# Zero products under the first loads, halved first loads, moments by piece, and a shorter inverse square root

## The chip, the cores and the metric

The kernel runs on one core of one Trainium2 chip. The metric is the device time of one execution in microseconds. The kernel before was timed three times: 1588.16, 1591.35 and 1591.58 us, a median of 1591.35 us. One more execution was recorded by the profiler; all profile lines in this document that are said to be of before come from that one.

The core has five engines with an instruction stream each: TensorE (PE in the profile; its weight loads are PEld), VectorE (DVE), ScalarE (ACT), GpSimd (POOL) and SyncE (SP), which here issues most of the transfers. An engine executes its own stream in order and waits for others by semaphores.

## The reference

The input is x of shape (4, 1024, 256) in float32, 4096 tokens of 256 values. Two layers follow, each of a mixing part and a feed-forward part, and each part is wrapped in a residual sum and a layer norm without scale and shift:

```
x = layernorm(x + L0_attn(x))   # state-space mixing, 2 heads of 128, state 64
x = layernorm(x + L0_ffn(x))    # 256 -> 1024, exact GELU, -> 256
x = layernorm(x + L1_attn(x))   # 16 heads of 16, 64 positive features, causal linear attention
x = layernorm(x + L1_ffn(x))    # 2 shared experts, and 2 of 8 routed experts per token, SiLU-gated, hidden 512
layernorm(x) = (x - mean) / sqrt(var + 1e-5)      over the 256 values of a token
L1_attn:  q, k are divided by max(norm, 1e-12) per head before the features
```

Four layer norms and the norms of q and k each need an inverse square root; these are what the changed function `rsqrt` computes. The first mixing part starts with `dtBC = x @ W_xproj.T`, the first matrix product of the program.

## The kernel before, in words

**Tiling.** Tokens are cut into NBLK = 8 blocks of TB = 512, a block into NT = 4 tiles of P = 128 tokens. `xs[i]` holds block i with tokens on the partitions (128 x 4 x 256) and is updated in place through all parts; `xts[i]` holds its transpose from the host (128 x 2 x 512), of which only the first products make use. Everything is float32. PE executes such a product of 512 columns as two instructions, and the profile counts both.

**Order of the work.** PE's instructions stand in an order that the program writes out: each piece of work is a `Task` with an assumed cost, a rank and waiting times behind others, and `trace_tasks` (line 243) picks the next one by these. The streams of the other engines in that stage are put in order by the compiler's scheduler, from its own estimate of each instruction's time. So DVE, ACT and POOL streams can change in places that a diff does not touch, while PE's does not. In the last stage (from line 1239) PE, DVE and ACT all keep the written order.

**Opening (lines 119 to 175).** SP issues, in order: the weights `wx_sb` (128 x 2 x 2 x 128: chunk of the 256 input values, product number, column), `xts[0]`, the small vector `vec0` copied to all partitions, `xts[2]`, `xts[4]`, `xts[6]`, the even `xs`, and the rest. ACT loads a function table and computes `neg_a` (line 172), which needs `vec0`. `ssd_block` (line 269) then begins with `project(0)` and `project(1)` (line 283), two products each that add up over the two chunks k; ACT copies each result out of PSUM (line 285), and `steps` (line 287) turns the first with four transposes into `ps_dtb` (line 291). DVE works out the step sizes from it (lines 299 to 312).

**Inverse square roots.** `rsqrt(v, shape, tag)` (line 178) takes a first estimate from the bits of v (a shift, line 182, and a subtraction from a constant, line 183) and improves it with three Newton steps of three DVE instructions each (lines 185 to 187). It is called 49 times: by `layernorm` (line 206) 24 times on 128 x 4 values, after the first mixing, the first feed-forward part and the attention, once for each block; by `attn_front` (line 508) 16 times on 128 x 64 values; and by `last_norm` (line 1064) 9 times on 128 x 4, 128 x 3 or 128 x 1 values. Each instruction needs the one before.

**After the first layer.** Attention (`attn_front`, `attn_back`, `attn_tail`) runs interleaved with the first feed-forward part of other blocks and with the shared experts (`shared_jobs`, line 920). Then tokens are sorted by expert, and the routed part (`slot_tiles`, line 998) runs 71 tiles of 128 tokens, whose results are added into `acc` in memory.

**Last stage (lines 1239 to 1268).** `combine` (line 1058) loads each block's part of `acc` back and POOL adds it to `xs[i]` (line 1062), eight times. Meanwhile PE runs the shared experts for the blocks 6 and 7: for each block eight `hidden` pieces (ps_g, line 938; SiLU on ACT, line 946; product on DVE, line 947) and four `output` pieces (ps_e, line 956; added to x on DVE, line 965). The counter n numbers these pieces, 0 to 23; the pieces 20 to 23 are the outputs of block 7's four tiles. The last norms are spread between the pieces: `last_norm(i, tiles)` gives three functions, `sums` (two DVE instructions for each tile: moments, lines 1075 and 1076), `scales` (lines 1080 to 1082, with `rsqrt`) and `finish` (ACT, line 1086, and the store, line 1090). Blocks 0 to 6 take one function after each of three pieces. For block 7 the first three tiles' `sums` and `scales` come after piece 22, `finish` after piece 23, and then the fourth tile is done by itself.

The functions that the change touches, and what calls them:

## Time and profile before

| what | value |
|---|---|
| median of three runs | 1591.35 us (1588.16 to 1591.58) |
| the profiled execution | 1590.25 us |
| its span, first to last instruction | 1588.5 us |
| mean granted PE clock | 0.988 of full |
| PE, DVE, ACT, POOL busy, share of the span | 95%, 48%, 38%, 35% |
| instructions of DVE | 2383 |
| PE's first product | at 5.06 us |

The profile's page gives the busy time of each engine, the span in forty slices, the chain of work that ended last (followed back from the last instruction, at each step to what released it) and the costliest groups of instructions. A timeline gives start and duration of each instruction and, in brackets, how long its engine was idle before it and what ended the wait. The granted clock is what the throttle let PE have, in parts of full speed. DVE instructions overlap their neighbours a little, so what counts for a chain of dependent ones is the time from start to start.

### The profile page before, as it was taken

The numbers are of one execution on the slowest core, as the hardware profiler recorded it, in microseconds if no ns is written. First come the engines' busy times: TensorE is split into PE (matmuls) and PEld (weight loads), VectorE is DVE, ScalarE is ACT, GpSimd is POOL, SyncE is SP. The second block draws the span as 40 slices with busy tenths as digits, with TensorE's granted clock in tenths as the row PEclk, the third lists the DMA queues.
The fourth block names the chain that finished last, engine by engine and source line by source line (L and its number), as shares of the span: only waits on it lengthen the run. The fifth ranks groups of instructions, "written<-read, shape, count | busy, mean of one in ns | idle before, by whom it ended". The sixth has DMA issues, their size and how long they took to land.

```text
span 1588.5 us, 25546 instructions
## 1 busy us (share of the span) xinstructions
PE 1505.6 (95%) x9744; PEld 973.1 (61%) x9744; DVE 768.2 (48%) x2383; ACT 600.9 (38%) x1061; POOL 557.8 (35%) x531
## 2 busy tenths in 40 slices
PE   8999989999998999899999999999999999999987
PEld 5575655656675767565667565565666666666544
DVE  6977824763656556655544437122222222222374
ACT  2555374354556363554545621102222222222132
POOL 5623323343433162614332204013444444443410
PEclk9999999999999999999999999999999999999999
DMA  9200000000000000200001034042322322322421
GB/s 345 85 1 1 1 1 1 14 15 1 27 2 14 15 1 28 94 28 15 28 2 41 2 105 160 14 143 38 47 46 45 47 46 45 47 45 33 123 73 47
DMA packets 48023, 74.08 MB, mean 47 GB/s; under 512 B 8512, under 2 KB 38464, under 8 KB 46368
## 3 DMA queue, kind: packets, MB, share of 16 engines
q1 hardware_dynamic: 33840, 52.19, 9.3%
q0 software_dynamic: 13632, 18.69, 7.6%
q8 instruction: 80, 1.31, 0.4%
q10 hardware_dynamic: 432, 1.57, 0.3%
q14 instruction: 39, 0.32, 0.1%
HBM read 46.19 MB, written 26.25 MB: 46 GB/s over the span
## 4 chain that ended last, share of the span: by engine, by line
PE 73%; DVE 13%; ACT 8%; POOL 3%; issue 2%; DMA 1%; SPq 0%; DVEq 0%; ACTq 0%; POOLq 0%
PE ps_ge L1008 15%; PE ps_g L938 9%; PE ps_ye L1030 8%; PE ps_e L956 6%; PE ps_h L436 5%; PE ps_f L448 5%; PE ps_sc L611 3%; PE ps_o L650 3%; PE ps_qk L497 2%; PE ps_gT L1023 2%; PE ps_bc L283 2%; PE ps_v L522 1%; PE ps_k L633 1%; PE ps_p L559 1%; PE ps_w L715 1%
## 5 line engine op out<-in xcount | busy, mean ns | idle before, releaser
L1008 PE MATMUL ps_ge<-w,xeT 128*128 x568 | 255.7, 593 | 1.0 <-issue 1.0
L938 PE MATMUL ps_g<-xTs,w 128*128 128x512 f32 x512 | 230.8, 603 | 12.6 <-ACT sl L946 6.7
L938 PEld LDWEIGHTS ps_g<-xTs,w 128*128 128x128 f32 x512 | 95.9, 192 | 126.1 <-issue 105.5
L1008 PEld LDWEIGHTS ps_ge<-w,xeT 128*128 128x128 f32 x568 | 102.4, 190 | 103.5 <-issue 103.5
L1039 POOL DMA_INDIRECT acc<-ye,back x71 | 112.5, 1584 | 112.2 <-DVE xew L995 77.0
L436 PE MATMUL ps_h<-xT,w_sb 128*128 128x512 f32 x256 | 125.3, 632 | 22.6 <-ACT hT L439 12.0
L983 POOL DMA_INDIRECT xe<-xt,sent x71 | 70.0, 986 | 216.6 <-PE ps_xe L991 154.1
L1018 DVE TENSOR_TENSOR ge<-se,ps_ge 128x512 f32<-128x512 f32 x71 | 48.8, 688 | 183.9 <-PE ps_ge L1008 181.0
L1030 PE MATMUL ps_ye<-w2e,geT 128*128 x568 | 134.4, 380 | 0.0
L956 PE MATMUL ps_e<-w,gT 128*128 128x256 f32 x512 | 116.7, 385 | 5.8 <-DVE x L965 3.0
L448 PE MATMUL ps_f<-w_sb,hT 128*128 128x256 f32 x512 | 118.1, 385 | 1.6 <-ACT hT L439 1.6
L956 PEld LDWEIGHTS ps_e<-w,gT 128*128 128x128 f32 x512 | 97.4, 193 | 24.3 <-DVE x L965 4.6
L1030 PEld LDWEIGHTS ps_ye<-w2e,geT 128*128 128x128 f32 x568 | 102.5, 190 | 12.2 <-ACT ye L1038 0.8
L448 PEld LDWEIGHTS ps_f<-w_sb,hT 128*128 128x128 f32 x512 | 96.6, 192 | 17.1 <-issue 2.8
L947 DVE TENSOR_TENSOR gT<-sl,ps_g 128x512 f32<-128x512 f32 x64 | 43.7, 686 | 118.3 <-PE ps_g L938 86.6
L436 PEld LDWEIGHTS ps_h<-xT,w_sb 128*128 128x128 f32 x256 | 49.1, 201 | 79.6 <-issue 49.9
L946 ACT ACTIVATE sl<-ps_g 128x512 f32<-128x512 f32 x64 | 37.9, 595 | 147.7 <-PE ps_g L938 138.8
L623 DVE TENSOR_TENSOR sc<-ps_sc,mask_le 128x512 f32<-128x512 f32 x96 | 62.6, 685 | 60.4 <-PE ps_sc L611 51.3
L1016 ACT ACTIVATE se<-ps_ge 128x512 f32<-128x512 f32 x71 | 42.4, 597 | 125.0 <-PE ps_ge L1008 125.0
L572 POOL TENSOR_SCALAR qf<-qf,csq 128x512 f32<-128x512 f32 x32 | 50.2, 1570 | 107.6 <-ACT qf L570 106.5
L621 POOL TENSOR_TENSOR sc<-sc,mask_le 128x512 f32<-128x512 f32 x32 | 40.9, 1279 | 113.9 <-ACT sc L620 113.6
L577 POOL TENSOR_SCALAR qf<-qf,csq 128x512 f32<-128x512 f32 x32 | 65.2, 2038 | 15.9 <-ACT qf L575 13.0
(251 smaller groups left out, 2578.1 us busy)
## 6 DMA issues: line engine op xcount, KB each, us to landing
w<-in_moe SPq DMA_DIRECT2D x8, 1024.0 KB, 8.7
xt<-in_xT SPq DMA_DIRECT2D x8, 512.0 KB, 9.9
x<-in_x SPq DMA_DIRECT2D x8, 512.0 KB, 10.3
acc<-zero SPq DMA_DIRECT2D x16, 256.0 KB, 4.8
xt<-x SPq DMA_DIRECT2D x8, 512.0 KB, 3.6
td<-xTr SPq DMA_DIRECT2D x16, 256.0 KB, 2.5
w2e<-in_moe SPq DMA_DIRECT2D x8, 512.0 KB, 7.4
part<-acc SPq DMA_DIRECT2D x8, 512.0 KB, 7.2
```

The lines of the kernel that those rows point to most:

```text
L436: nc.tensor.matmul(ps, w1_sb[:, k, m * P : (m + 1) * P], v.xT[:, k, :], start=(k == 0), stop=(k == KC - 1))
L448: nc.tensor.matmul(v.ps[:, j % 2, :], v.hT[:, m, j * P : (j + 1) * P], w2_sb[:, m, :], start=(m == 0), stop=(m == HID0 // P - 1),)
L572: nc.gpsimd.tensor_scalar_mul(f, f, csq)
L577: nc.gpsimd.tensor_scalar(f, f, CLIP_LO, csq, ALU.max, ALU.mult)
L623: nc.vector.tensor_mul(t_s, ps_s, mask)
L938: nc.tensor.matmul(ps[s], w[e][:, 2 * s + k, m * P : (m + 1) * P], xT[i][:, k, :], start=(k == 0), stop=(k == KC - 1),)
L956: nc.tensor.matmul(ps, gT[i, e][:, m, j * P : (j + 1) * P], w2e[:, m, :], start=(e == 0 and m == 0), stop=(e == NSH - 1 and m == HID // P ...
L983: nc.gpsimd.indirect_dma_start(out=xe, out_offset=None, in_=xt, in_offset=bass.IndirectOffsetOnAxis(ap=sent[:, s : s + 1], axis=0),)
L1008: nc.tensor.matmul(pg[a], xeT[s][:, k, :], w13[:, bass.ds(e * (4 * HID) + (2 * a + k) * HID, HID)], start=(k == 0), stop=(k == KC - 1),)
L1018: nc.vector.tensor_mul(ge[s], se, pg[1])
L1030: nc.tensor.matmul(ps[:, :D], geT[s][:, m, :], w2[:, bass.ds(of[s] * (2 * HID) + m * D, D)], start=(m == 0), stop=(m == HID // P - 1),)
L1039: nc.gpsimd.indirect_dma_start(out=acc, out_offset=bass.IndirectOffsetOnAxis(ap=back[:, s : s + 1], axis=0), in_=ye, in_offset=None, compu ...
```

## The change

There are four parts.

1. PE's stream gets two products of a tile of zeros (128 x 512, set by DVE) with itself, ahead of the first `ssd_block`; their result is never read.
2. The loads of `wx_sb` and `xts[0]` are halved. `wx_sb` is halved by product number, and the first half is issued on ACT; `xts[0]` is halved by chunk. In the built program ACT issues its half before the table load, and SP issues `xts[0]` chunk 0, `wx_sb` second half, `xts[0]` chunk 1, then `vec0` and the rest as before.
3. `rsqrt` takes after the same first estimate one step of third order and one Newton step, in nine DVE instructions altogether instead of eleven. A scale factor of 0.375 that the first step leaves out is put into the second step's constants.
4. The moments of the last block's first three tiles are taken one by one after the pieces 20, 21 and 22, instead of all three after 22. For that `last_norm` gets a flag `split`.

```diff
-    nc.sync.dma_start(out=wx_sb, in_=wx)
-    nc.sync.dma_start(out=xts[0], in_=xT[0])
+    for n in range(2):
+        (nc.scalar, nc.sync)[n].dma_start(out=wx_sb[:, :, n, :], in_=wx[:, :, n, :])
+        nc.sync.dma_start(out=xts[0][:, n, :], in_=xT[0][:, n, :])
     nc.sync.dma_start(out=vec0, in_=vecs[:NVEC0].partition_broadcast(P))
...
         nc.vector.tensor_scalar(r.bitcast(I32), s.bitcast(I32), -1.0, float(0x5F3759DF), ALU.mult, ALU.add)
-        for _ in range(3):
-            nc.vector.scalar_tensor_tensor(s, r, -0.5, r, ALU.mult, ALU.mult)
-            nc.vector.tensor_mul(s, s, v)
-            nc.vector.scalar_tensor_tensor(r, s, 1.5, r, ALU.add, ALU.mult)
+        nc.vector.tensor_mul(s, r, r)
+        nc.vector.tensor_mul(s, s, v)
+        nc.vector.scalar_tensor_tensor(s, s, -10.0 / 3.0, s, ALU.add, ALU.mult)
+        nc.vector.scalar_tensor_tensor(r, s, 5.0, r, ALU.add, ALU.mult)
+        nc.vector.scalar_tensor_tensor(s, r, -0.5 * 0.375**3, r, ALU.mult, ALU.mult)
+        nc.vector.tensor_mul(s, s, v)
+        nc.vector.scalar_tensor_tensor(r, s, 1.5 * 0.375, r, ALU.add, ALU.mult)
         return r
...
-    def last_norm(i, tiles):
+    def last_norm(i, tiles, split=False):
...
+        st = sm.tile([P, NT, 6], F32, tag="ln_st", name=f"ln_st{i}_{tiles[0]}")
+
         def sums():
-            st = sm.tile([P, NT, 6], F32, tag="ln_st", name=f"ln_st{i}_{tiles[0]}")
             for k, j in enumerate(tiles):
-                nc.vector.bn_stats(st[:, k, :], xs[i][:, j, :])
-                nc.vector.bn_aggr(mv[:, k, :], st[:, k, :])
+                moments(k, j)
+
+        def moments(k, j):
+            nc.vector.bn_stats(st[:, k, :], xs[i][:, j, :])
+            nc.vector.bn_aggr(mv[:, k, :], st[:, k, :])
...
+        if split:
+            return moments, scales, finish
         return sums, scales, finish
...
     with tc.manual_schedule(engines={mybir.EngineType.PE}):
+
+        idle = wkf.tile([P, TB], F32, name="idle")
+        nc.vector.memset(idle, 0.0)
+        ps = bank("ps_idle", 0)
+        for _ in range(2):
+            nc.tensor.matmul(ps, idle[:, :P], idle, start=True, stop=True)
         for i in range(NBLK):
             ssd_block(i, wk0)
...
+            if n == 20:
+                ends = last_norm(NBLK - 1, whole[:-1], True)
+            if 20 <= n < 23:
+                ends[0](n - 20, n - 20)
             if n == 22:
-                ends = last_norm(NBLK - 1, whole[:-1])
-                ends[0]()
                 ends[1]()
```

## The prediction

> **What bounds the kernel now.** I read the page first: busy time, then the chain that ended last. TensorE (PE) is busy for 95% of the span, and most of the chain is its work; the other engines come in only where PE waits.

> ```profile
> PE 1505.6 (95%) x9744; PEld 973.1 (61%) x9744; DVE 768.2 (48%) x2383; ACT 600.9 (38%) x1061; POOL 557.8 (35%) x531
> PE 73%; DVE 13%; ACT 8%; POOL 3%; issue 2%; DMA 1%; SPq 0%; DVEq 0%; ACTq 0%; POOLq 0%
> ```

> So the change can win only some 80 us of PE waits, or slow-clock PE time. It touches four stretches. First the timeline of the opening (start, duration, engine, line):

> ```profile
> 1.25 0.42 SPq L120 DMA_DIRECT2D xt<-in_xT  x1
> 5.06 5.83 PE L283 MATMUL ps_bc<-xt,wx_sb 128*128 128x512 f32 x8 [5.06 <-DMA xt<-in_xT]
> 7.75 0.33 PEld L283 LDWEIGHTS ps_bc<-xt,wx_sb 128*128 128x128 f32 x1 [0.52 <-issue]
> 7.99 0.20 ACT L172 ACTIVATE neg_a<-vec 128x2 f32<-128x2 f32 x1 [5.92 <-DMA vec<-in_vecs]
> 8.61 0.33 PEld L283 LDWEIGHTS ps_bc<-xt,wx_sb 128*128 128x128 f32 x1 [0.52 <-issue]
> 8.85 0.58 ACT L285 COPY bc<-ps_bc 128x512 f32<-128x512 f32 x1 [0.65 <-PE ps_bc L283]
> 9.44 0.19 PEld L283 LDWEIGHTS ps_bc<-xt,wx_sb 128*128 128x128 f32 x1 [0.50 <-issue]
> 9.87 0.19 PEld L283 LDWEIGHTS ps_bc<-xt,wx_sb 128*128 128x128 f32 x1 [0.24 <-issue]
> ```

> To see: PE waits 5.06 us for the load; its instructions then come 0.86 us apart (7.75 to 8.61) and only from 9.44 on 0.43 apart. A weight load takes 0.33 us before, 0.19 after. That is half clock, although the page's clock row says 9 there. ACT's first copy stands behind `neg_a`, which waits for the small vector load until 7.99.

> Then the stretch after the routed part, where POOL adds eight times (2.34 us each, 1497.81 to 1516.28):

> ```profile
> 1511.74 2.26 DVE L185 SCALAR_TENSOR_TENSOR ln_s<-ln_r 128x4 f32<-128x4 f32 x1
> 1514.04 2.26 DVE L186 TENSOR_TENSOR ln_s<-ln_s,ln_v 128x4 f32<-128x4 f32 x1
> 1516.33 0.16 DVE L187 SCALAR_TENSOR_TENSOR ln_r<-ln_s,ln_r 128x4 f32<-128x4 f32 x1
> 1517.79 0.69 DVE L947 TENSOR_TENSOR gT<-sl,ps_g 128x512 f32<-128x512 f32 x1
> 1518.53 3.45 PE L938 MATMUL ps_g<-xTs,w 128*128 128x512 f32 x4 [5.21 <-DVE gT L947]
> ```

> A 0.16 us step of the inverse square root lasts 2.26 us while POOL adds; PE waits 5.21 us for the product queued behind, then runs 4 instructions at half clock (granted clock 0.52 from 1518 to 1520).

> Last the chain at the end (start, length):

> ```profile
> 1577.36 0.34 DVE ln_st L1075
> 1579.00 0.18 DVE ln_v L1080
> 1581.54 0.34 DVE x L965
> 1585.10 0.60 ACT x L1086
> ```

> From 1577.36 the end hangs on DVE alone: three pairs of moments, a root, the last add, one more pair, one more root.

> **The change, part by part.** The sum is made against the profiled execution: 1590.25 us (span 1588.5), 1.1 below the median 1591.35 of runs from 1588.16 to 1591.58.

> *Start.* Removed: half clock. Added: a DVE memset of 128x512 ahead of two small ones that nobody needs before 930 us. Nearest rows: POOL's memset of that size 0.51 us, DVE's two of 128x16 0.11; taking 0.5, it ends at 0.86+0.5 = 1.4. PE's two zero products are four instructions of 0.86: 1.5 to 4.9. The loads: wx landed at 3.6, xt at 4.92; the halves bring the same bytes, but the last is issued a slot later (1.72 for 1.25), so it lands at 5.4 at worst. If the clock is up by then, the eight real instructions need 8x0.43 = 3.4 us and end near 8.4, not 10.89. When is it up? After the two slow starts shown, 3.1 us (1518.5 to 1521.6) to 4.4 us (5.06 to 9.44) after the first instruction: 4.6 to 5.9. But the vector load is now SP's fourth issue, 2.18 for 1.72, so `neg_a` runs at 8.45 at worst, ACT's copy at 8.7 to 9.3, and PE's `ps_dtb` transposes start at 9.3 instead of 10.89: -1.5. Ends: -2.1 (five slow instructions x 0.43, all kept), +0.5 (one issue slot late, nothing won). Next late is xt2, landing at 9.3 and now perhaps 9.8, when PE wants it at 9.75: no further gain, no loss. The load issued on ACT (0.4 us by SP's row) pushes its 1.28 us table load to 2.5; ACT waits until 8 anyway. Later loads go out 0.46 later; PE's only wait for a load in the whole trace is the first, so 0. Each load's issue waits for the one eight earlier; for the first x load that is now the first load, landed long before it is due.

> [...]

> *Roots.* 49 calls (24 norms of two layers, 16 of q and k, 9 last) have 9 DVE instructions for 11. A dependent step costs 0.20 us from start to start at 128x4, 0.26 at 128x64, so 0.4 to 0.5 a call. Over all 49 that is some 20 us of DVE, of which only what lies on the path counts. Adding up the chain's pieces on lines 182 to 187 before 900 us: 169 pieces, 37.4 us, of which 11 long ones held by POOL take 11.6, the other 158 take 25.8. POOL's holds do not shrink. 2/11 of 25.8 is 4.7 us if all of it reached PE. Half is my value, -2.4: there PE waits 22 us on DVE in some eighteen gaps (3.67 at 255, 1.96 at 491), but several end on ACT right behind, and interleaved steps cost only 0.07 of chain each. Against it stands the scheduler's new order on ACT, by the built program: near 63, 128 and 149 us a norm's four ACT instructions (2.07) go ahead of a decay, a copy and a Gelu. At 149 the Gelu `hT` ends at 151.7 for 149.1, just when PE wants its bank (151.8); the next decay slips by 0.3. At 128 the step chain behind the copy starts 0.6 later. At 63 the decay's consumer waits until 67.15 anyway. POOL swaps `qk` scaling ahead of one `qf` scaling at 717 and 808; `qkn_r` is ready there (715.2, 805.3): 0. Ends for this part: -5.5 (all 4.7 and some 0.8 by order) and +2.1 (no gain, one norm in front of PE).

> *After the routed part.* During POOL's adds the same five steps are held; multiplies are held as line 186 shows. After 1516.3 six remain instead of eight: -0.39 for `gT` and PE's wait. The next root (1521.4 to 1523.5) is also before what PE waits for at 1526.81 (1.38 us): again -0.39. Together -0.8; ends -0.4 and -2.3 (if the shorter wait also spares the half-clock stretch, 3.1x0.48 = 1.5).

> *End.* Two pairs of moments (0.53 each) move to where DVE idles 3.8 and 3.0 us; were that cover gone, each add would slip 0.6. The three tiles' scales are then done at 1580.1 for 1581.5, before PE's last product (1577.42+3.72 = 1581.14): the last add starts at 1581.2 for 1581.46, -0.3; the last root -0.4. Together -0.7 (ends -0.4, -1.1). The 3.4 us from 1585.10 to the end stay.

> Sum: -1.5 -2.4 -0.8 -0.7 = -5.4: 1590.25-5.4 = **1584.9 us**.

> **Rivals.**
> 1. The middle gives nothing: 1587.3, with the norm ahead of the Gelu up to 1589.4. For it: DVE is in order, the 11 holds remain, ACT ends 12.0 us of PE's waits on `hT`. Against: 255, where only norm steps and two clamps stand before `xT`.
> 2. Zero products do not raise the clock, or too late: start 0 instead of -1.5, 1586.4. For: no row shows PE on zeros. Against: the clock rose within 4.4 us of work both times.
> 3. Half-clock stretches go as well. The granted clock falls in 11 stretches, 19.1 us lost by the 3 us windows after the start, 1.7 each. Two or three shorter waits sparing it: 1580.5.
> 4. Slower: the clock falls at more places. It fell after waits of 0.43 and 0.39 us (764, 765) and of 0.29 and 0.81 (344, 346) but not after 2.05 (369) or 1.96 (491), so which gap trips it hangs on where the gap falls, and every gap moves now. Each costs 1.7; it decides from five extra stretches (8.6 us), 1593.4 and up. For: twelve waits over 1.3 us stand where the clock held. Against: the runs before spread by 3.4 us only.

> **How the numbers follow.** My case 0.50, rival 1 0.24, rival 2 0.09, rival 3 0.10, rival 4 0.07. About 0.2%, 3.2 us, is what a measurement of this kernel tells from no change: faster means below 1588.2. My case, 2 and 3 are faster and of rival 1 its better end, 0.06; same is the rest of rival 1; slower is rival 4. The range 1580.3 to 1589.6 takes in rivals 1, 2 and 3 and leaves out rival 4 and the far ends of the sums; the start's and middle's unknowns make its width.

> **What would show it.** `ps_dtb` first at 9.3 (10.1 if the clock is late, 10.9 if zeros do nothing), instructions 0.43 apart from 6 on; PE's wait near 1518 at 4.8 for 5.2; last add directly behind PE; steps at 255 and 166 to 191 shorter, and total PE waits before 900 down by 2 to 3 us. Wrong it would be by new waits of `ps_h` for `hT` near 145, or more windows with a clock near 0.5.

## The result

The change makes the kernel a little faster. In the first comparison the median is 1583.86 us (1582.07 to 1584.61, 6 runs) against 1588.65 before (1588.16 to 1591.58, 6 runs), a ratio of 0.9963 with an interval of 0.9950 to 0.9976. Measured again, beside three of the experiments, it was 1581.90 against 1589.67: 0.9951 (0.9937 to 0.9965). The forecast was 1584.9 with a range of 1580.3 to 1589.6. The profiled execution took 1583.58 us (span 1581.9), 6.67 less than the one before.

The page of the changed kernel, its busy times and the shares of the chain that ended last:

```profile
PE 1507.4 (95%) x9748; PEld 973.6 (62%) x9748; DVE 753.6 (48%) x2286; ACT 601.8 (38%) x1061; POOL 557.9 (35%) x531
...
PE 75%; DVE 12%; ACT 8%; POOL 2%; issue 1%; DMA 0%; DVEq 0%; ACTq 0%; POOLq 0%
```

PE's time without work, span less busy time, falls from 82.9 to 74.5 us. Of these 8.4, 3.6 are the zeros, which now fill PE's first wait (1.51 to 5.08); the rest is waits that have gone. DVE has 97 instructions fewer (two a root, one memset more).

The opening (start, duration, engine, line; what the idle time before it ended on):

```profile
1.51 3.78 PE L1154 MATMUL ps_idle<-idle 128*128 128x512 f32 x4 [1.51 <-DVE run L850]
1.97 0.58 SPq L121 DMA_DIRECT2D xt<-in_xT  x1
...
4.23 0.34 PEld L288 LDWEIGHTS ps_bc<-xt,wx_sb 128*128 128x128 f32 x1 [0.52 <-DMA wx_sb<-in_wx]
...
6.42 0.71 PEld L288 LDWEIGHTS ps_bc<-xt,wx_sb 128*128 128x128 f32 x2 [1.00 <-DMA xt<-in_xT]
7.59 0.19 PEld L288 LDWEIGHTS ps_bc<-xt,wx_sb 128*128 128x128 f32 x1 [0.47 <-issue]
...
8.69 0.20 ACT L173 ACTIVATE neg_a<-vec 128x2 f32<-128x2 f32 x1 [5.93 <-DMA vec<-in_vecs]
...
9.74 0.60 PE L296 MATMUL ps_dtb<-ident,bc 128*128 128x128 f32 x4
```

PE is busy from 1.51, but waits for the second half of the x load until 6.42. Weight loads are short, that is, the clock is up, only from 7.59, and `neg_a` still waits for the vector load. `ps_dtb` starts at 9.74; before it was 10.72.

After the routed part, and at the end:

```profile
1508.96 2.27 DVE L187 TENSOR_TENSOR ln_s<-ln_s,ln_v 128x4 f32<-128x4 f32 x1
1511.26 0.16 DVE L188 SCALAR_TENSOR_TENSOR ln_s<-ln_s 128x4 f32<-128x4 f32 x1
...
1512.32 0.69 DVE L952 TENSOR_TENSOR gT<-sl,ps_g 128x512 f32<-128x512 f32 x1
...
1513.06 3.54 PE L943 MATMUL ps_g<-xTs,w 128*128 128x512 f32 x4 [4.57 <-DVE gT L952]
...
1575.33 0.42 DVE L970 TENSOR_TENSOR x<-ps_e,x 128x256 f32<-128x256 f32 x1 [0.96 <-PE ps_e L961]
...
1578.58 0.60 ACT L1095 ACTIVATE x<-x,ln_v,ln_r 128x256 f32<-128x256 f32 x1 [2.54 <-DVE ln_v L1091]
```

As many steps as before are held by POOL, but fewer remain behind, so PE waits 4.57 us for 5.21; the four products behind still run at half clock (3.54 us; granted clock 0.50 from 1513 to 1515). At the end the last add now waits for PE (0.96) and not for DVE's moments.

How far the changed kernel is ahead at the same PE instruction (its start before less its start after; the places are times of the changed kernel): 1.0 us at `ps_dtb`, 1.8 at 136, 3.25 at 188, 4.9 at 225, 6.55 at 527; then it loses 1.5 at 561 and 0.5 at 633, stays at 4.8 to 4.9 up to 1489, and gains 1.0 behind the routed part and 0.75 at the end. The 1.7 us from 188 to 225 are half clock that the profile before has there and this one has not.

### The profile page after: what moved, and what is told of

It is laid out like the page before. It is cut to its first block, busy times and chain, and to the rows that moved or that the text cites. A ratio compares the mean times of both kernels' runs of the same rounds, so it can differ in the third digit from the quotient of the medians.

```text
span 1581.9 us, 25458 instructions
## 1 busy us (share of the span) xinstructions
PE 1507.4 (95%) x9748; PEld 973.6 (62%) x9748; DVE 753.6 (48%) x2286; ACT 601.8 (38%) x1061; POOL 557.9 (35%) x531
## 4 chain that ended last, share of the span: by engine, by line
PE 75%; DVE 12%; ACT 8%; POOL 2%; issue 1%; DMA 0%; DVEq 0%; ACTq 0%; POOLq 0%
PE ps_ge L1013 15%; PE ps_g L943 10%; PE ps_ye L1035 8%; PE ps_e L961 6%; PE ps_h L441 5%; PE ps_f L453 5%; PE ps_o L655 3%; PE ps_sc L616 3%; PE ps_qk L502 2%; PE ps_gT L1028 2%; PE ps_v L527 2%; PE ps_bc L288 2%; PE ps_k L638 1%; PE ps_p L564 1%; PE ps_w L720 1%
## 5 line engine op out<-in xcount | busy, mean ns | idle before, releaser
L951 ACT ACTIVATE sl<-ps_g 128x512 f32<-128x512 f32 x64 | 38.0, 597 | 149.1 <-PE ps_g L943 140.0
## 6 DMA issues: line engine op xcount, KB each, us to landing
xt<-in_xT SPq DMA_DIRECT2D x7, 512.0 KB, 10.9
```

## The experiments

All times are medians; "before" was run beside each group and stood at 1589.65, 1589.67, 1590.02 and 1590.12 us in the four groups. Single executions of one kernel differ by several us (those of before lay between 1585.4 and 1596.1), so a profile shows where time goes, and only the medians what a kernel takes.

### One part at a time

**The start alone.** The kernel before, with the halved loads and

```diff
+        idle = wkf.tile([P, TB], F32, name="idle")
+        nc.vector.memset(idle, 0.0)
+        ps = bank("ps_idle", 0)
+        for _ in range(2):
+            nc.tensor.matmul(ps, idle[:, :P], idle, start=True, stop=True)
```

> The kernel before with the zero products and the split loads alone; roots and moments as before. Theory (the middle's gain comes from shorter roots): the first ps_dtb transposes start at 9.7 us for 10.7, and this lead of 1.0 us is carried to the end or partly lost in the first waits; time 0.5 to 1.3 us below before, waits before 900 us as before. Rival (the middle's gain is one of moved gaps, set off by the earlier start): the lead grows to 3 us or more by 320 us although the roots are old, because other waits fall and the half-clock stretch near 222 us goes; time 3 us or more below before.

Measured: 1587.63 us, ratio 0.9988 (0.9975 to 1.0001). `ps_dtb` started at 10.36, not 9.74, because the vector load landed later in this execution (`neg_a` at 9.54 for 8.69). The lead does not grow to 3 us in the middle: up to 1489 us it is 2.1 at most, and 1.7 of that are half clock that the profile before has behind 138 us and this one has not. By the medians the start is worth 2.0 us, by the interval anything from 4 us to nothing, and the lead at `ps_dtb` is 0.4 us in this profile.

**The roots alone.** The kernel before with the nine-instruction root in place of

```diff
-        for _ in range(3):
-            nc.vector.scalar_tensor_tensor(s, r, -0.5, r, ALU.mult, ALU.mult)
-            nc.vector.tensor_mul(s, s, v)
-            nc.vector.scalar_tensor_tensor(r, s, 1.5, r, ALU.add, ALU.mult)
```

> The kernel before with the new inverse square root alone; opening and moments as before. Theory: the parts add up, so this gives the middle's -3.9 us (lead of 1.5 between 166 and 191 us, and the half-clock stretch near 222 us gone), -0.9 after the routed part and -0.4 at the end, in all about -5 us, ps_dtb still at 10.7. Rival: without the earlier start the gaps fall elsewhere, the half-clock stretch near 222 stays, and the losses of 1.5 us at 561 and 0.5 us at 633 stay or grow: -1 to -3 us.

Measured: 1582.70 us, ratio 0.9956 (0.9940 to 0.9973). As far as the intervals tell, that is all of the gain; this one reaches from 4.3 to 9.5 us and takes in the theory's 5. Where the time leaves the path is the same as in the whole change: near 190, 225, 345 and 501 us (times of the kernel before), with the same losses at 566 (1.46) and 637 (0.51).

**The moments alone** (the `split` flag of `last_norm`, its callers as changed):

> The kernel before with the last tiles' moments by piece alone. Theory: the three pairs of moments leave the end's chain, but the old root is 0.4 us longer, so the last add starts directly or nearly directly behind PE: -0.2 to -0.4 us, and nothing before 1560 us is changed: PE's instructions start at the same times within 0.1 us up to there. Rival: the moments by piece each sit ahead of an add that PE or ACT waits for, and the end is later by up to 0.6 us.

Measured: 1589.98 us, ratio 0.9997 (0.9983 to 1.0011). No gain of 0.2 to 0.4 us can be seen in the median or excluded at this width. The profile's end did as foretold: the last add starts 0.42 us after the start of PE's last instruction, where it was 0.70. But with the roots alone it is 0.42 too, so that beside the shorter root the moments bring nothing that the profiles show. The expectation that nothing moves before 1560 us was wrong for one execution against another: with the same order up to there this profile is 5 us ahead at the end, since four half-clock stretches of the profile before (138, 222, 717 and 765 us) were missing in it and one more came (311).

**The change without zeros** (the tile and its memset go too)

```diff
-        for _ in range(2):
-            nc.tensor.matmul(ps, idle[:, :P], idle, start=True, stop=True)
```

> The changed kernel without the products of zeros and their memset; split loads, roots and moments as changed. Theory: the zeros raise the clock, so without them the first eight real instructions all or nearly all run 0.86 us apart, full clock from about 9 us on, ps_dtb at 10.5 to 11 us for 9.74, and the time is 0.8 to 1.2 us above the changed kernel. Rival (the second half of the x load and neg_a set the start, the zeros add little): ps_dtb at 9.7 to 10.0 all the same, and the same time within 0.3 us.

Measured: 1581.32 us, ratio 0.9947 (0.9926 to 0.9968). The clock and `ps_dtb` were later than the theory said, and yet the time is not higher. The opening without zeros:

```profile
4.09 2.08 PE L288 MATMUL ps_bc<-xt,wx_sb 128*128 128x512 f32 x2 [4.09 <-DMA wx_sb<-in_wx]
...
6.79 5.49 PE L288 MATMUL ps_bc<-xt,wx_sb 128*128 128x512 f32 x6 [0.62 <-DMA xt<-in_xT]
...
12.07 0.92 PE L296 MATMUL ps_dtb<-ident,bc 128*128 128x128 f32 x4
```

`ps_dtb` is at 12.07, 1.35 later than before the change: the halved loads bring PE's first work forward to 4.09, but the last half lands at 6.8, where the whole load had landed by 5.06, and the products behind it still start slow (0.86 us apart up to 12.07).

### Which half of the opening, and how much a step is worth

Four kernels on one chip: the changed one, the one with the opening as before, the one with whole loads and zeros, and the one with a still shorter root.

```diff
 f2_opening:  - zeros; - halves;  + nc.sync.dma_start(out=wx_sb, in_=wx) and (out=xts[0], in_=xT[0])
 f3_whole:    - halves;           + nc.sync.dma_start(out=wx_sb, in_=wx) and (out=xts[0], in_=xT[0])
 f4_two_newton, in rsqrt:
-        (the seven lines of the two new steps)
+        for _ in range(2):
+            nc.vector.scalar_tensor_tensor(s, r, -0.5, r, ALU.mult, ALU.mult)
+            nc.vector.tensor_mul(s, s, v)
+            nc.vector.scalar_tensor_tensor(r, s, 1.5, r, ALU.add, ALU.mult)
```

> The changed kernel itself, to stand beside the three others on one chip. Both theories: about 0.35 to 0.45% below before, 1582.5 to 1584.5 us; the start's transposes ps_dtb between 9.7 and 10.4 us, by when the vector load and the second half of the x load land.

> The changed kernel with the opening as before: no zero products, whole loads; new roots and moments by piece. Theory (the roots are nearly all of it, and the opening is worth what ps_dtb shows, 0.4 to 1.4 us): ps_dtb at 10.7 to 11.5 us, and the time 0.4 to 1.4 us above the changed kernel. Rival (the opening's shift is absorbed by the first waits between 50 and 200 us): the same time as the changed kernel within 0.4 us.

> The changed kernel with the first two loads whole again, zero products kept. Theory (the split delays the last piece, 6.4 to 6.8 us for 5.0, and the vector load behind it; the zeros raise the clock about 6.1 us after PE's first instruction whatever the loads do): PE runs on real products from 5.0 without a gap, three slow ones to 7.6, five fast ones to 9.7, ps_dtb at 9.7, neg_a at 8.0; 0 to 0.7 us below the changed kernel. Rival (the split feeds PE earlier and is what brings the gain): ps_dtb at 10.3 or later and the time 0.5 to 1 us above the changed kernel.

> The changed kernel with the old root cut to two of its three Newton steps (relative error about 5e-6): 8 DVE instructions a root, one fewer than the changed kernel, three fewer than before. Theory (what the root costs is its number of dependent steps ahead of PE): the two steps removed so far brought 4 to 6 us, so one more brings 2 to 3 us: 1580.5 to 1582 where the changed kernel is at 1583.5. Rival (the gain is one of order and of where the gaps fall): the time moves by less than 1 us either way or up.

| kernel | median, us | ratio to before | `ps_dtb` at, us | PE without work, us |
|---|---|---|---|---|
| changed | 1581.90 | 0.9951 (0.9937 to 0.9965) | 10.41 | 75.3 |
| opening as before | 1582.24 | 0.9950 (0.9936 to 0.9964) | 10.17 | 77.8 |
| whole loads, zeros | 1581.98 | 0.9950 (0.9937 to 0.9964) | 9.84 | 75.3 |
| root of 8 instructions | 1583.10 | 0.9956 (0.9938 to 0.9975) | 10.41 | 73.7 |

The opening, in any of its forms, cannot be told from the one before by the time. With the opening as before, `ps_dtb` came at 10.17 and not at 10.7 or later, and the time is within the rival's 0.4 us of the changed kernel. What holds `ps_dtb` in the changed opening is seen in the group's own profile of the changed kernel:

```profile
5.08 3.78 PE L288 MATMUL ps_bc<-xt,wx_sb 128*128 128x512 f32 x8
9.59 0.20 ACT L173 ACTIVATE neg_a<-vec 128x2 f32<-128x2 f32 x1 [6.84 <-DMA vec<-in_vecs]
...
10.41 0.63 PE L296 MATMUL ps_dtb<-ident,bc 128*128 128x128 f32 x4 [1.55 <-ACT bc L290]
```

PE is done with its eight products at 8.9 and waits 1.55 us for ACT's copy, which stands behind `neg_a`. The vector load behind the halves lands late: `neg_a` starts at 9.36 to 9.68 in eight of the nine profiles with halved loads and at 8.69 in the first; with whole loads it is 7.39 to 8.11 in five. The zeros raise the clock early, and the halves bring a new wait in its place. With whole loads and zeros `neg_a` is at 7.39, PE is the last again and `ps_dtb` starts at 9.84, 0.14 later than foretold.

The root of 8 instructions was to bring 2 to 3 us and did not. Its profile shows PE 2.6 us ahead of the changed kernel's in the same group, but 1.5 of that are half clock behind 138 us that this execution was spared; PE's time without work is 1.6 us less. The median is no lower all the same: its runs spread from 1579.24 (granted clock 0.990) to 1587.50 (0.984), and four of the seven are above 1583. The longer runs are those with the lower clock, so half clock may have taken what the shorter waits gave. Whether it falls more often in this kernel, and why, is open.

### What in the root counts, and where

**Two idle steps behind the new root**, 11 instructions again:

```diff
         nc.vector.scalar_tensor_tensor(r, s, 1.5 * 0.375, r, ALU.add, ALU.mult)
+        nc.vector.tensor_scalar_max(r, r, 0.0)
+        nc.vector.tensor_scalar_max(r, r, 0.0)
         return r
```

> The changed kernel with two further DVE steps behind each root (a maximum with zero, twice, which changes no value), so that a root has 11 instructions again as before; the built order of PE, ACT and POOL is then that of the kernel with the changed opening and the old root. Theory (the gain hangs on how many dependent steps a root has, with the order that the scheduler makes of that): the middle's gain goes, 1587 to 1589.5 us, PE's waits together back up by 4 us or more, the txT wait of 1.5 us near 190 us is there again. Rival (the new kinds of steps are what is faster): 1581.5 to 1584 us.

Measured: 1589.82 us, ratio 0.9996 (0.9984 to 1.0008). The whole gain of the change is gone with two steps, PE's time without work is back at 80.8 us (75.3), and the wait at 190 us is back (1.74). So the kind of the steps is worth nothing that can be measured; what counts is their number, with the order that the scheduler makes of it. The two were not separated. This kernel keeps the new opening and the moments by piece, so these two together are worth 0.6 us by the ratio and 2.5 at most.

**The old root for q and k only** (`rsqrt_old` is the function as it was before)

```diff
-            rn = rsqrt(ss, [P, NJ * 2 * NH], "qkn").rearrange("p (j h) -> p j h", j=NJ)
+            rn = rsqrt_old(ss, [P, NJ * 2 * NH], "qkn").rearrange("p (j h) -> p j h", j=NJ)
```

> The changed kernel with the old root of 11 instructions for q and k (16 of the 49 calls) and the new one for the norms. Theory (the norms bring all of it; the q and k root only shifts POOL's scaling of qk, which holds DVE's clamps at 633 us): the same as the changed kernel within 0.8 us, and the clamp of kf near 628 us is held for about 0.75 us instead of 1.24, PE's wait there 1.6 for 2.1. Rival (a third of the calls, and wider ones, bring their share): 2 us or more above the changed kernel.

Measured: 1584.53 us, ratio 0.9966 (0.9954 to 0.9978). The time alone does not decide: the ratio is 0.0003 and 0.0015 above the changed kernel's two, which were measured in other groups, and the intervals overlap. But PE's time without work is 77.0 us, against 74.5 and 75.3 in the changed kernel, so by the profiles the q and k roots, a third of the calls, carry some 2 us, and the theory fell. The clamp near 628 us was indeed held for 0.74 us instead of 1.24 and PE waited 1.63 for 2.11, but that is the smaller matter. The larger one is at 190 us. DVE in the kernel before:

```profile
188.76 0.23 DVE L185 SCALAR_TENSOR_TENSOR qkn_s<-qkn_r 128x64 f32<-128x64 f32 x1
189.02 0.23 DVE L186 TENSOR_TENSOR qkn_s<-qkn_s,ss 128x64 f32<-128x64 f32 x1
189.28 0.23 DVE L187 SCALAR_TENSOR_TENSOR qkn_r<-qkn_s,qkn_r 128x64 f32<-128x64 f32 x1
189.42 0.68 DVE L456 TENSOR_TENSOR x<-ps_f,x 128x512 f32<-128x512 f32 x1
```

Two q and k roots run one behind the other on DVE from 178 us on, and right behind the second stands the add of `ps_f` to x that releases PE's transposes. PE's transposes there, in the kernel before, in the changed one, and with the old q and k root:

```profile
190.16 0.66 PE L201 MATMUL ps_txT<-ident,x 128*128 128x128 f32 x4 [1.56 <-DVE x L456]
```

```profile
186.91 0.66 PE L206 MATMUL ps_txT<-ident,x 128*128 128x128 f32 x4 [0.16 <-DVE x L461]
```

```profile
188.92 0.66 PE L218 MATMUL ps_txT<-ident,x 128*128 128x128 f32 x4 [1.44 <-DVE x L473]
```

The wait falls from 1.56 to 0.16 with the shorter root and is back at 1.44 where only q and k have the long one. From the first step of the first root to the add, DVE takes 10.83 us in the kernel before and 9.57 in the changed one. Four steps of 0.26 us are 1.04 of these 1.26 us. Held steps differ too: in the second root, POOL's scaling of the first qk holds two of the first steps in the kernel before (0.83 and 0.76) and one of them in the changed kernel (0.76).

**The lost 1.5 us at 561.** POOL's add of `b2` in halves:

```diff
-                nc.gpsimd.tensor_add(xs[i], xs[i], b2)
+                for h in range(2):
+                    at = slice(2 * h, 2 * h + 2)
+                    nc.gpsimd.tensor_add(xs[i][:, at, :], xs[i][:, at, :], b2[:, at, :])
```

> The changed kernel with POOL's addition of b2 to x (128x1024, about 2 us, eight times) cut into two additions of 128x512; the order of the instructions on PE, ACT and DVE is unchanged. Theory (the 1.5 us lost again near 561 us are DVE's clamp of kf held for 2.09 us by this addition): the clamp there takes at most 1.3 us, PE's wait for qk falls from 1.23 to 0.4 us or less, and PE's lead over the kernel before is 0.8 to 1.4 us larger after 566 us than in the changed kernel's profile with the same lead before it; time 0.3 to 1.4 us lower. Rival (the hold is not this addition, or the second half holds the clamp as long): the clamp stays at 2 us and the time is the same.

The place in the kernel before, in the changed one (second group's profile), then with halves:

```profile
564.51 0.80 DVE L579 TENSOR_SCALAR kf<-kf 128x512 f32<-128x512 f32 x1
...
564.98 2.19 POOL L444 TENSOR_TENSOR x<-x,vec 128x1024 f32<-128x1024 f32 x1
```

```profile
560.53 2.00 POOL L449 TENSOR_TENSOR x<-x,vec 128x1024 f32<-128x1024 f32 x1
560.73 2.08 DVE L584 TENSOR_SCALAR kf<-kf 128x512 f32<-128x512 f32 x1
...
564.06 1.98 PE L502 MATMUL ps_qk<-wqkv_sb,xTa 128*128 128x512 f32 x4 [1.22 <-DVE qk L505]
```

```profile
559.99 2.33 POOL L451 TENSOR_TENSOR x<-x,vec 128x512 f32<-128x512 f32 x2
560.19 1.18 DVE L586 TENSOR_SCALAR kf<-kf 128x512 f32<-128x512 f32 x1
...
562.62 1.98 PE L504 MATMUL ps_qk<-wqkv_sb,xTa 128*128 128x512 f32 x4 [0.32 <-DVE qk L507]
```

The clamp starts 0.2 us behind POOL's add and lasts as long as that add does: 2.08, or 1.18 with half of it; PE's wait falls from 1.22 to 0.32 us. So the hold is this addition. In the kernel before the same clamp started 0.47 ahead of the addition and took 0.80. The roots' gain was lost again here because DVE and POOL had moved against each other by 0.67 us. The profile with halves gains 0.9 us on the changed kernel's at this place, as foretold. The time does not show it: 1583.05 us, ratio 0.9961 (0.9946 to 0.9975), an interval too wide to show or exclude 0.3 to 1.4 us.

### Zeros where PE waits

```diff
                 ps = bank(f"ps_h{i}_{m}", 1)
+                for _ in range({2: 2, 3: 4, 5: 2}.get(i, 0) if m == 0 else 0):
+                    nc.tensor.matmul(ps, idle[:, :P], idle, start=True, stop=True)
```

> The changed kernel with products of zeros also in three of PE's waits for xT ahead of a block's first ps_h product: 2, 4 and 2 products (1.7, 3.4 and 1.7 us at full clock) near 137, 251 and 407 us, where the changed kernel's profile shows waits of 1.97, 3.67 and 1.92 us and half clock behind each; the order of the instructions on ACT, DVE and POOL is unchanged. Theory (half clock follows a gap on PE, and zeros hold the clock there as they raised it at the start): the granted clock stays at 1.0 behind the three places, the eight ps_h instructions at 251 take 3.4 to 3.8 us for 5.3, and each place gives about 1.7 us: 3 to 5 us below the changed kernel, 1577 to 1580 us. Rival (the falls move to the next gaps, or the zeros only take PE's place and delay the real products): as many half-clock stretches as before, near 20 us in all, and 1581 to 1584 us.

Measured: 1585.79 us, ratio 0.9978 (0.9969 to 0.9987). That is above the changed kernel's second ratio, 0.9951 (0.9937 to 0.9965), and above its first, 0.9963, with intervals that overlap. The three places went two ways. The first and the second:

```profile
134.93 1.98 PE L441 MATMUL ps_h<-idle 128*128 128x512 f32 x4
136.75 3.65 PE L443 MATMUL ps_h<-xT,w_sb 128*128 128x512 f32 x8
...
249.10 6.61 PE L441 MATMUL ps_h<-idle 128*128 128x512 f32 x8 [3.67 <-DVE xT L208]
255.55 3.60 PE L443 MATMUL ps_h<-xT,w_sb 128*128 128x512 f32 x8
```

At 135 the zeros run in the gap, the clock stays at 1.00, and the lead over the changed kernel's profile in the second group grows by 1.75 us (0.60 to 2.35). That the zeros held the clock is not shown by this one profile: of the thirteen without zeros there, with waits of 1.74 to 1.99 us, four kept full clock as well. At 249 and 408 the zeros waited 3.67 and 1.92 us themselves, as long as the real products had. They then ran at half clock (granted 0.50; 6.61 us for eight instructions) and delayed the real ones by 6.4 and 3.5 us. The zeros do not read `xT`, so they did not wait for data. Most likely they waited for the bank that they write to, which the copy of `xT` out of PSUM, named as releaser, was still reading. I had taken that wait for one on data alone. Zeros in a bank of their own, or at 135 alone, were not tried.

## Why the prediction was right

The time and the sign were right; the terms of the sum were not all. That the sum came out near is partly luck: the start brought less than forecast, the roots more.

**Start, -1.5.** Mis-sized: -1.0 in the changed kernel's profile, and between nothing and 2 us by the medians, never clear of noise (alone 0.9988; with the new roots 1581.90 with it and 1582.24 without). Two bounds failed. The second x half was to land "at 5.4 at worst" and came at 5.8 to 6.8, and `neg_a` was to run "at 8.45 at worst" and ran at 8.69 to 9.68. Three of the four halves took 0.58 to 0.68 us to issue where I had a slot of 0.46, so the vector load behind them went out at 2.59 and not at 2.18. In eight of nine profiles it landed a further 0.5 to 0.8 us late, and why is open. So rival 2's result, nothing from the start, is not excluded. Of its two grounds the second, that the clock comes too late, is partly true: it came later than the forecast 4.6 to 5.9 us, clearly so in five of nine profiles. The first is not, for zeros do raise the clock: the first short weight load came 3.3 to 6.1 us after PE's first instruction in nine profiles with zeros (4.8 to 7.6 us from the span's start; in two of them within 0.6 us of the first real product), and 3.5 to 6.1 after it in four without zeros and with whole loads (8.45 to 11.06). In the one with halves and no zeros it came 8.6 us after, with a wait of 0.62 us on the way.

No run shows the term from which the forecast's 10.1 us for `ps_dtb` with a late clock is worked out; in the nine profiles with zeros the clock rose as given above, 3.3 to 6.1 us after PE's first instruction, and `ps_dtb` started at 9.74 to 10.41.

**Roots in the middle, -2.4.** The term that was mis-sized: the roots alone give 7 us in all by their ratio, and with two idle steps added nothing is left. From the profiles of four kernels with the old number of steps and six with the new, PE's time without work falls by 5.1 us (82.4 to 77.3, openings without zeros) or 4.8 (79.8 to 75.0, with zeros); 1.8 and 1.0 of that lie behind the routed part and at the end, so the middle gives 3.3 or 3.8, not 2.4. I took half of 2/11 of the chain's root time, an average. The path is not average: most roots are hidden, and where two stand one behind the other in front of what PE needs, all of their four steps count, and a held step with them. The interval of the time, 4.3 to 9.5 us, takes in the waits' 5 us; whether there is more is not settled. My direct expectation at 255 failed: the wait for `xT` is 3.51 to 3.67 us in all fourteen profiles, 3.67 in the changed kernel's. It ends on a copy by DVE, here in the kernel before and in the changed one:

```profile
254.57 0.69 DVE L203 COPY xT<-ps_txT 128x512 f32<-128x512 f32 x1
```

```profile
249.64 0.69 DVE L208 COPY xT<-ps_txT 128x512 f32<-128x512 f32 x1
```

In both kernels eight steps of the norm's root stand ahead of this copy on DVE, and the fifth of them is held for 2.0 us by POOL's addition of `b2`. Behind the copy stand three more steps in the kernel before and one in the changed kernel. So the two spared steps lie behind what PE waits for. What I said about 145 held: no new wait came there.

**After the routed part, -0.8; end, -0.7.** Both near the forecast: PE's waits fell by 0.64 (5.21 to 4.57) and 0.48 (1.38 to 0.90), and the end gained 0.75 with the last add directly behind PE. Over the four profiles with the old number of steps and the six with the new, the first wait is 5.09 and 4.70 on average: 0.39, just as forecast. The second varies with either (0.59 to 1.38 and 0.59 to 0.90). Of the end's gain 0.28 us come with the moments alone or the roots alone (the last add, above), and 0.38 with the shorter last root (3.26 us from the last add to ACT's last instruction, 3.64 before); so the root alone would have given nearly all of it.

**Rivals.** The first, that the middle gives nothing, is excluded by the roots alone and by the padded root. Its ground, that ACT's waits on `hT` stay at 12.0 us, failed too: they are 9.5 in the changed kernel, 12.0 again with padding. The third, half-clock stretches spared, is partly true. One wait shows it, 1.57 us for `hT` in front of `ps_f`, in the padded kernel and in the changed one of the second group:

```profile
223.43 5.41 PE L455 MATMUL ps_f<-w_sb,hT 128*128 128x256 f32 x16 [1.57 <-ACT hT L446]
```

```profile
221.39 3.72 PE L453 MATMUL ps_f<-w_sb,hT 128*128 128x256 f32 x16 [1.57 <-ACT hT L444]
```

The wait is the same, and the products behind it run at half clock in one (granted 0.50 from 225 to 227) and at full clock in the other (1.00): 1.7 us. All profiles with the new q and k root spare this stretch; four of the five with the old one have it. But others came (483 to 488, 495, 507), and PE's busy time over all is on average the same with old and new roots within 1 us. So the third rival's mechanism moved time about and did not set the result; the fourth's extra stretches came too, and were mostly given back by the `hT` waits behind them.

## What to carry to other kernels

A chain of small dependent steps costs where it stands in front of what the critical engine needs, and two such chains in a row cost twice the steps (near 190, 1.04 of the 1.26 us spared on DVE; PE's wait there fell from 1.56 to 0.16): find those places and count the steps that stand ahead of the wait's end, instead of taking a share of an average. Steps spared behind it bring nothing (PE's wait for `xT` near 250 is 3.67 us in both kernels). Work without use that is to hold PE's clock must depend on nothing that the real work waits for, most likely its PSUM bank included: zeros that waited 3.67 us themselves delayed the products behind them by 6.4. And where a POOL instruction lengthens a DVE one that starts behind it (the clamp near 561: 2.08 us, and 0.80 where it started ahead), a gain of a microsecond in front can be lost behind, because the order of two starts turns; look for steps that have become long where the code has not changed.
